# A graph attention layer on one core: 58 tiles of raw node rows are gathered while the node table is built

## The chip, the core and the metric

One core of a Trainium2 chip. The metric is device microseconds of one execution. The kernel before takes 4131.94 us, the median of three runs (4130.94 to 4132.53). Five engines work side by side, each through its own list of instructions in order: PE (TensorE, matrix products), DVE (VectorE), ACT (ScalarE), POOL (GpSimd) and SP (SyncE, which only issues transfers here). They wait for one another by semaphores.

## The reference

There are 12,500 nodes with 128 features and 412,500 edges, sorted by their target, with 64 features each; 4 heads of 32.

```python
h = relu(layernorm(x))                       # 12500 x 128
h = h @ W_node.T;  e = edge_attr @ W_edge.T  # per head: 32 columns
att = sum(concat(h[src], h[dst], e) * a)     # one logit per edge and head
att = where(att > 0, att, 0.2 * att)
m = maximum(segment_max(att, dst), 0)
ex = exp(att - m[dst])
denom = segment_sum(ex, dst) + (num_edges - deg) * exp(-m)
out = x + segment_sum(ex / denom[dst] * h[src], dst)
```

## The kernel before, in words

**The table.** The kernel first builds, in device memory, a `table` with one row of 144 numbers per node: for each head the 32 projected features, two columns of ones and the node's own logits towards source and target. Then it walks over the edges in 66 batches (`NBT`) of 7 chunks of 896 edges (49 tiles of 128 edges each; less in the last batch), gathers the table row of each edge's source node, works out the weights, and sums the weighted rows per target on PE.

**The lead-in** (`lead_in`, L432) builds the table from 98 tiles of 128 nodes (`NB`), loaded and written in 14 groups (`sizes`, L305), mostly of 9 tiles; a unit is 3 tiles of a group. A group's x rows are loaded by SP (`load_rows`, L307). DVE takes the statistics of each tile (`measure`, L329), combines them per group (`combine`, L334, four instructions), ACT takes the root (`root`, L344), and DVE makes the scale and the shift (`deviate`, L349, two instructions). A unit is then normalized (`normalize`, L355: its first tile on ACT, the other two on POOL), turned on PE (`turn`, L368), taken through ReLU on the way out of PSUM (`keep_turned`, L373: the first tile on ACT, the other two on DVE), multiplied with the weights on PE (`project`, L382), copied out by ACT (`keep_rows`, L387), and POOL sets its columns of ones (`set_ones`, L394). A group's rows are written to the table by an ACT transfer (`write`, L398), and POOL copies its target logits (`keep_logits`, L402).

The order of these steps on each engine comes from a list scheduler at the end of `lead_in`: a `Step` has an engine, a duration and a lag in ns, the steps it stands behind, and a rank; the step that can start first by these numbers is emitted next, the rank deciding between equals. The numbers only set the order; the engines wait by semaphores.

Behind the lead-in stand `keep_near` (L406: the target logits are turned and written to device memory) and `chunk_ranges` (L513), in which DVE works out, for all chunks at once, where each begins.

**The batches** (L1089 on). `gather` (L660) issues one indirect transfer on POOL per tile of 128 edges: 128 rows of the table, found through a column of the batch's index tile `ends` (`index`, L232). The gathered rows lie in `hs`, one of four buffers (`RING`); the first two, `opening` and `second`, are set apart before the lead-in, the other two come after it. Batches 0 and 1 are gathered without any wait but that for the table and the indices; from batch 4 on a small memset (`gate`, L663) in front of a batch's gathers waits until PE has done the sums of the batch four before it. DVE waits for a batch's rows in `weigh` (L738; a wait on a counting semaphore), makes the logits and weights, marks targets (`mark`, L719), and multiplies the rows by the weights in `scatter` (L846), whose matrix products sum them. `choose` (L628) picks each edge's target logits, and `begin` (L706) makes the edge features' part of the logits on PE.

Ahead of the lead-in POOL sets constants (L186 to L215: `logits`, `pen_sb`, `marks`, `carry`).

Of the kernel before, what the change touches and what calls it, by code (L numbers as in the profile page):

```python
# [49 lines left out]
ACTS = 1  # L50
# [76 lines left out]
def kernel(  # L127
# [58 lines left out]
    nc.gpsimd.memset(logits, 0.0)  # L186
    pen_sb = const.tile([R, 2, CE + 1], F32, name="pen_sb")
    nc.gpsimd.memset(pen_sb, 0.0)
# [4 lines left out]
    nc.gpsimd.memset(lowest, 0.0)  # L193
    nc.gpsimd.memset(highest, float(NQ))
    for b0, n, b in parts():
        c = chunk_of(b + 1)
        if c < NCH:
            nc.gpsimd.memset(lowest[:, c:c + 1], float((b0 + n) * (P // W)))
    for b in range(NBT):
        if b == NBT - 1 or base_of(b + 1) > base_of(b):  # L200
            c = chunk_of(b + 1) - 1
            nc.gpsimd.memset(highest[:, c:c + 1], float(base_of(b) + WQ - 2))
    for at in sorted({base_of(b) for b in range(NBT)}):
        of = [b for b in range(NBT) if base_of(b) == at]
        nc.gpsimd.memset(bases[:, chunk_of(of[0]):chunk_of(of[-1] + 1)], float(at))

# [6 lines left out]
    nc.gpsimd.memset(carry_m, 0.0)  # L213
    carry = const.tile([P, AW - 1], F32, name="carry")
    nc.gpsimd.memset(carry, 0.0)  # L215
# [22 lines left out]
    with (  # L238
# [6 lines left out]
    ):  # L245
        wn = p1.tile([P, D], F32, name="wn")
# [60 lines left out]
        def load_rows(b0, n):  # L307

            s = Rows()
            s.b0, s.n = b0, n  # L310
# [4 lines left out]
            if full < n:  # L315
                nc.vector.memset(s.x[:, full, :], 0.0)
                rest = N - (b0 + full) * P
                nc.sync.dma_start(s.x[:rest, full, :], x[(b0 + full) * P:N, :])
            s.stats = p2.tile([P, XB, 2, 3], F32, name="stats", bufs=5)
# [34 lines left out]

        def normalize(u, own):  # L355
# [3 lines left out]
            for i in own:  # L359
                k = slice(u.i0 + i, u.i0 + i + 1)  # L360
                if i < ACTS:
                    nc.scalar.activation(u.hn[:, i, :], s.x[:, k, :].rearrange("p b d -> p (b d)"), AF.Identity,
                                         scale=s.rstd[:, k], bias=s.shift[:, k])
                else:
                    nc.gpsimd.tensor_scalar(u.hn[:, i, :], s.x[:, k, :].rearrange("p b d -> p (b d)"),
# [7 lines left out]
        def keep_turned(u, own):  # L373
            if u.hT is None:
                u.hT = p2.tile([P, XS, P], F32, name="hT", bufs=5)
            if own[0] < relu_acts(u):
                for i in own:
                    nc.scalar.activation(u.hT[:, i, :], u.pt[:, i, :], AF.Relu)
                return
            nc.vector.tensor_scalar(u.hT[:, own[0]:u.m, :], u.pt[:, own[0]:u.m, :], 0.0, None, op0=OP.max)  # L380
# [6 lines left out]
        def keep_rows(u):  # L387
            s = u.s
            if u is s.units[0]:
                s.rows = p3.tile([P, XB, ROW], F32, name="rows", bufs=4)  # L390
# [1071 lines left out]
```

## Time and profile before

| what | value |
|---|---|
| median of 3 runs | 4131.94 us |
| the profiled execution | 4131.72 us |
| its span, first to last instruction | 4129.9 us |
| mean granted TensorE clock | 0.658 |
| busy: DVE, POOL, PE, ACT | 58%, 75%, 33%, 11% |
| indirect gathers on POOL | 3223, mean 947 ns, from 63.3 us on |
| moved by the DMA engines | 457.10 MB, mean 111 GB/s |

The rows of the profile are read so: a group's row has its line, engine, operation, what it writes and reads, its count, then the busy time and the mean ns of one, then the idle time of the engine just before these instructions and what ended it. A timeline's row begins with the start and the duration in us. Engines with a small q (SPq, ACTq) are the issuing of transfers. "issue" is time in which an engine waited for nothing that the profile shows.

### The profile page before, as it was taken

Reading aid. Unit: us, or ns where it says so; the run is one execution under the profiler, and the core shown is the slowest. Engines: PE = TensorE matmul, PEld = TensorE weight load, DVE = VectorE, ACT = ScalarE, POOL = GpSimd, SP = SyncE. Lnnn points to the kernel's source line nnn. Section 1 sums busy time; section 2 is a strip of 40 time slices with the busy share of each in tenths; the row PEclk is TensorE's granted clock in tenths of the full one; section 3 lists DMA queues with packets and bytes.
Section 4 is the critical chain, followed back from the end, with each engine's and each line's share of the span. In section 5 each row is a group of like instructions: output and inputs, shape, how many; then the busy total and the mean of one; then the engine's idle time right before and its main releaser. Section 6 shows DMA issues by size and latency. Waiting matters only on the chain. (4 is left out here: it accounts for less than half of the span.)

```text
span 4129.9 us, 18410 instructions
## 1 busy us (share of the span) xinstructions
PE 1360.4 (33%) x3375; PEld 538.8 (13%) x3375; DVE 2390.1 (58%) x3503; ACT 461.0 (11%) x669; POOL 3100.1 (75%) x3457
## 2 busy tenths in 40 slices
PE   5333133233233323323323313323323332332332
PEld 4111011011011111101101101101111110110111
DVE  7446556556556556745655754654665654665576
ACT  4001101101101101101110110110110110110011
POOL 6777777777777777777777777777777777777775
PEclk8666666566566666666666666656666666666665
DMA  7433343343344344333434333434434434434432
GB/s 205 124 114 101 108 116 106 106 113 112 99 114 117 96 113 119 102 107 114 102 107 119 106 108 110 108 106 113 115 99 115 117 92 112 119 99 114 119 102 61
DMA packets 417255, 457.10 MB, mean 111 GB/s; under 512 B 240614, under 2 KB 324794, under 8 KB 417132
## 3 DMA queue, kind: packets, MB, share of 16 engines
q0 software_dynamic: 103136, 237.83, 21.8%
q1 hardware_dynamic: 200288, 165.86, 14.0%
q10 hardware_dynamic: 113708, 52.17, 4.6%
q14 instruction: 95, 0.78, 0.1%
q8 instruction: 28, 0.46, 0.0%
HBM read 406.51 MB, written 49.05 MB: 110 GB/s over the span
## 5 line engine op out<-in xcount | busy, mean ns | idle before, releaser
L667 POOL DMA_INDIRECT hs<-table,ends x3223 | 3053.1, 947 | 978.1 <-issue 974.7
L857 PE MATMUL pa<-hs,hot 128*128 128x504 f32 x1820 | 929.5, 676 | 2665.9 <-DVE hs L852 2665.9
L765 DVE TENSOR_TENSOR logits<-hs,pick 128x196 f32<-128x196 f32 x65 | 32.4, 499 | 1495.0 <-DVEq L684 1495.0
L857 PEld LDWEIGHTS pa<-hs,hot 128*128 128x128 f32 x1820 | 397.7, 223 | 3189.9 <-issue 3158.9
L852 DVE TENSOR_TENSOR hs<-hs,exr 128x1848 f32<-128x1848 f32 (+1 forms) x130 | 451.6, 3516 | 0.0
L780 ACT ACTIVATE both<-a 32x224 f32<-32x224 f32 (+2 forms) x268 | 103.2, 385 | 2591.6 <-DVE a L778 2589.3
L715 PE MATMUL z<-eft,wa 128*32 128x512 f32 (+1 forms) x792 | 320.0, 547 | 6.5 <-DMA eft<-in_ef 6.5
L642 DVE COPY_PREDICATED pick<-more,pick 128x1568 f32<-128x1568 int32 (+3 forms) x260 | 253.6, 975 | 8.9
L642 DVE COPY_PREDICATED pick<-more,lw 128x3136 f32<-128x3136 int32 x65 | 241.0, 3707 | 9.6 <-ACT pick L626 3.9
L626 ACT COPY pick<-lw 128x3136 f32<-128x3136 f32 x65 | 182.4, 2806 | 11.5 <-ACTq L684 10.0
L964 DVE TENSOR_TENSOR acc<-acc,up 128x70 f32 x461 | 105.2, 228 | 66.0 <-issue 51.1
L775 DVE TENSOR_TENSOR_SCAN up<-pen_sb,z 32x896 f32<-32x896 f32 (+1 forms) x67 | 133.6, 1994 | 2.3
L777 DVE TENSOR_TENSOR_SCAN m<-pen_sb,up 32x896 f32<-32x896 f32 (+1 forms) x67 | 132.6, 1979 | 2.3
L735 DVE TENSOR_TENSOR hot<-exr,key 128x1568 f32<-128x1568 f32 x65 | 116.4, 1791 | 2.3
L770 DVE TENSOR_TENSOR up<-z,zst 32x224 f32<-32x224 f32 (+2 forms) x268 | 104.3, 389 | 13.8
L715 PEld LDWEIGHTS z<-eft,wa 128*32 128x32 f32 x792 | 79.7, 110 | 242.1 <-issue 234.9
L782 DVE SCALAR_TENSOR_TENSOR both<-pen_sb,up 32x224 f32<-32x224 f32 (+2 forms) x268 | 100.1, 374 | 4.3
L894 ACT COPY r<-turned 128x245 f32<-128x245 f32 x65 | 41.4, 638 | 337.5 <-ACTq L684 294.4
L774 DVE TENSOR_TENSOR z<-up,a 32x896 f32<-32x896 f32 (+1 forms) x67 | 72.3, 1079 | 2.3
L778 DVE TENSOR_TENSOR a<-z,m 32x896 f32<-32x896 f32 (+1 forms) x67 | 71.7, 1070 | 2.3
L773 DVE TENSOR_SCALAR a<-up 32x896 f32<-32x896 f32 (+1 forms) x67 | 71.3, 1064 | 2.3
L712 PE MATMUL z<-eft,wa 128*64 128x512 f32 (+1 forms) x132 | 64.6, 572 | 21.6 <-DMA eft<-in_ef 21.6
(182 smaller groups left out, 901.5 us busy)
## 6 DMA issues: line engine op xcount, KB each, us to landing
eft<-in_ef SPq DMA_DIRECT2D x33, 1792.0 KB
hs<-table,ends POOLq DMA_INDIRECT x3223, 2.5
eft<-in_ef SPq DMA_DIRECT2D x33, 1344.0 KB
wide<-stage ACTq DMA_DIRECT2D x65, 504.0 KB, 2.9
lw<-near SPq DMA_DIRECT2D x461, 64.0 KB
pen_sb<-pens SPq DMA_DIRECT2D x66, 98.1 KB
xg<-in_x SPq DMA_DIRECT2D x52, 112.0 KB
table<-rows ACTq DMA_DIRECT2D x8, 648.0 KB
```

The lines of the kernel that those rows point to most:

```text
L626: nc.scalar.copy(s.pick[:, :, :s.chunks, :], lw[:, None, :s.chunks, :n].to_broadcast([P, T, s.chunks, n]))
L642: nc.vector.copy_predicated(s.pick[:, :, :s.chunks, :n], bit[:, :, :, None].to_broadcast([P, T, s.chunks, n]), more)
L667: load = nc.gpsimd.indirect_dma_start(out=s.hs[:, t * CB + q, :], out_offset=None, in_=table[:, :], in_offset=bass.IndirectOffsetOnAxis(ap ...
L715: s.made = own_half(s, nc.tensor.matmul(s.z[:, part], wa3[:, j + s.b % 2 * (SB + 1), :], s.eft[:, j, part], start=False, stop=(j == NEXT - ...
L735: nc.vector.tensor_tensor(s.hot.rearrange("p t q r -> p (t q) r"), rows_ps[:, None, :].to_broadcast([P, T * CB, W]), key[:, :, None].to_br ...
L770: on_half(s, nc.vector.tensor_tensor(grouped(up, g), grouped(s.z, g), zst[g * R:(g + 1) * R, t0:t1, :], op=OP.add))
L775: on_half(s, nc.vector.tensor_tensor_scan(up[:, e0:e1], s.pen[:, e0:e1], z, 0.0, op0=OP.add, op1=OP.max))
L777: nc.vector.tensor_tensor_scan(mp[:, ::-1], s.pen[:, e1:e0:-1], up[:, e0:e1][:, ::-1], 0.0, op0=OP.add, op1=OP.max)
L780: nc.scalar.activation(both[g * R:(g + 1) * R, 0, t0:t1, :], grouped(att, g), AF.Exp)
L852: nc.vector.tensor_tensor(rows, rows, ex_ps[:, t0:t1, :CB * H, None].to_broadcast([P, t1 - t0, CB * H, HB]), op=OP.mult)
L857: scattered[s.b] = nc.tensor.matmul(wide_ps[:, g, :], s.hot[:, t, g * NEXT:g * NEXT + SB, :].rearrange("p q r -> p (q r)"), flat[:, at:at ...
L964: nc.vector.tensor_tensor(sums, sums, put[:, i0 + i, :, :], op=OP.add)
```

## The change

The rows of the whole first batch (49 tiles) and of the first 9 tiles of the second (`RAW = (49, 9)`) are no longer gathered from the table. POOL gathers the edges' raw x rows (512 bytes of x in place of 576 bytes of the table) straight into the two `hs` buffers as soon as the first index tile is there, while the table is being built. These 58 tiles then go through the lead-in in place, as 7 further groups behind the table's 14: they are normalized, turned, projected, and `keep_rows` writes the 144 columns over the raw rows. They are not written to the table, and they have no target logits to keep.

POOL has no other share in the lead-in any more: the normalization of its two tiles goes to ACT, but for the first tile of each third unit, which DVE takes; ReLU is all on DVE, three tiles in one instruction; the ones and the logits' copies go to DVE. POOL's constants move behind its raw gathers. The first use of the weights moves into a step of its own, `prepare`. `gather` skips the tiles that are there already, and `weigh` of batch 0 has no wait on a counting semaphore.

```diff
-ACTS = 1
+RAW = (T * CB, XB)
...
+    def set_constants():
+        nc.gpsimd.memset(carry, 0.0)
...
+        early = [index(0)]
+        raw = [pool.tile([P, T * CB, ROW], F32, name="hs") for pool in (opening, second)]
+
+        def gather_raw(k):
+            for i in range(RAW[k]):
+                nc.gpsimd.indirect_dma_start(
+                    out=raw[k][:, i, :D], out_offset=None, in_=x[:, :],
+                    in_offset=bass.IndirectOffsetOnAxis(ap=early[k][:, i % CB, 0, i // CB:i // CB + 1], axis=0))
+
+        gather_raw(0)
...
+            at = b0 - NB
+            if at >= 0:
+                s.rows = raw[0][:, at:at + n, :] if at < RAW[0] else raw[1][:, at - RAW[0]:at - RAW[0] + n, :]
+                s.x = s.rows[:, :, :D]
+                return parted(s)
...
+        def of_vector(u):
+            return (u.s.b0 + u.i0) // XS % 3 == 0 and u.m == XS
...
-                if i < ACTS:
+                if i or not of_vector(u):
                     nc.scalar.activation(u.hn[:, i, :], s.x[:, k, :].rearrange("p b d -> p (b d)"), AF.Identity,
                                          scale=s.rstd[:, k], bias=s.shift[:, k])
                 else:
-                    nc.gpsimd.tensor_scalar(u.hn[:, i, :], s.x[:, k, :].rearrange("p b d -> p (b d)"),
+                    nc.vector.tensor_scalar(u.hn[:, i, :], s.x[:, k, :].rearrange("p b d -> p (b d)"),
                                             s.rstd[:, k], s.shift[:, k], op0=OP.mult, op1=OP.add)
...
+        def keep_turned(u):
+            u.hT = p2.tile([P, XS, P], F32, name="hT", bufs=5)
+            nc.vector.tensor_scalar(u.hT[:, :u.m, :], u.pt[:, :u.m, :], 0.0, None, op0=OP.max)
...
-            nc.gpsimd.memset(rows.rearrange("p b (h k) -> p b h k", h=H)[:, :, :, HD:HD + 2], 1.0)
+            nc.vector.memset(rows.rearrange("p b (h k) -> p b h k", h=H)[:, :, :, HD:HD + 2], 1.0)
...
-            nc.gpsimd.tensor_copy(tn[:, s.b0:s.b0 + s.n, :],
+            nc.vector.tensor_copy(tn[:, s.b0:s.b0 + s.n, :],
...
+        tables = len(sizes)
+        sizes += [min(XB, n - i) for n in RAW for i in range(0, n, XB)]
...
-            if len(groups) == len(sizes):
+            if len(groups) == 3:
+                early.append(index(1))
+                gather_raw(1)
+                set_constants()
+            if len(groups) == tables:
                 early.extend(index(b) for b in range(2, AHEAD))
...
+                if g >= tables:
+                    steps["landed", g] = Step("gathered", 1250 * n, 5000, [], g, lambda: None)
+                    steps["load", g] = Step("none", 0, 0, behind + [("landed", g), ("load", g - 1)], g, load_next)
...
-        s.hs = rings[s.b % RING].tile([P, T * CB, ROW], F32, name="hs")
+        s.hs = raw[s.b] if s.b < 2 else rings[s.b % RING].tile([P, T * CB, ROW], F32, name="hs")
...
-                if t < tiles_of(s.c0 + q):
+                if t < tiles_of(s.c0 + q) and t * CB + q >= (RAW[s.b] if s.b < 2 else 0):
                     s.tiles.append((t, q))
```

How the order on the engines moves, at three places. First POOL at the end of the lead-in, before (`tn` holds the target logits, `rows` a group's table rows, `hs` a batch's gathered rows):

```order
L403 COPY tn<-rows 128x24
L396 MEMSET rows 128x12x2
L403 COPY tn<-rows 128x12
L396 MEMSET rows 128x8x2
L403 COPY tn<-rows 128x8
L667 DMA hs<-table,ends 128x144 x196
L663 MEMSET gate 128x1
L667 DMA hs<-table,ends 128x144 x49
```

And POOL with the change, from its second iota on:

```order
L164 IOTA pid_c 128x1
L253 DMA hs<-in_x,ends 128x128 x58
L201 MEMSET carry 128x34
L202 MEMSET carry_m 128x1
L203 MEMSET pen_sb 32x1794
L204 MEMSET logits 128x224
```

```order
L217 MEMSET marks 1x21
L217 MEMSET marks 1x6
L699 DMA hs<-table,ends 128x144 x138
L695 MEMSET gate 128x1
L699 DMA hs<-table,ends 128x144 x49
```

The normalizations, ones and copies are gone from POOL; 58 gathers of x and then the constants stand in their place, and of the 196 gathers in front of the first gate 138 are left. The raw gathers also carry waits, here with the semaphores' names (`DMAHW` counts plain transfers, `DMASW` POOL's; eight of each are used in turn):

```order
L253 DMA hs_131<-in_x,ends_129 128x128 [waits DMAHW1_49]
L253 DMA hs_131<-in_x,ends_129 128x128 x7
L253 DMA hs_131<-in_x,ends_129 128x128 [waits DMASW0_49]
L253 DMA hs_131<-in_x,ends_129 128x128 [waits DMASW1_49]
L253 DMA hs_131<-in_x,ends_129 128x128 [waits DMASW2_49]
```

From the ninth on each waits for the transfer that used its semaphore last, the one eight before. Next DVE in the middle of the table, for about one group of nine, before (`stats`, `tot`, `dif`: statistics; `shift`, `rstd`: scale and shift; `pt`, `hT`: a turned unit before and after ReLU):

```order
L351 RECIPROCAL rstd_475<-rstd_475 128x9
L353 SCALAR_TENSOR_TENSOR shift_495<-tot_424,rstd_475 128x9
L337 TENSOR_TENSOR tot_497<-stats_272 128x18
L339 TENSOR_TENSOR dif_499<-stats_272 128x9
L340 SCALAR_TENSOR_TENSOR dif_499<-dif_499 128x9
L341 TENSOR_TENSOR dif_499<-dif_499,tot_497 128x9
L332 BN_STATS stats_315<-xg_313 128x6 x6
L380 TENSOR_SCALAR hT_529<-pt_518 128x256
L332 BN_STATS stats_315<-xg_313 128x6 x3
L380 TENSOR_SCALAR hT_551<-pt_535 128x256
```

And with the change (`hn`: a normalized unit):

```order
L374 RECIPROCAL rstd_532<-rstd_532 128x9
L376 SCALAR_TENSOR_TENSOR shift_547<-tot_488,rstd_532 128x9
L360 TENSOR_TENSOR tot_553<-stats_327 128x18
L362 TENSOR_TENSOR dif_555<-stats_327 128x9
L363 SCALAR_TENSOR_TENSOR dif_555<-dif_555 128x9
L364 TENSOR_TENSOR dif_555<-dif_555,tot_553 128x9
L391 TENSOR_SCALAR hn_559<-xg_302,rstd_532,shift_547 128x128
L355 BN_STATS stats_384<-xg_382 128x6 x3
L417 MEMSET rows_526 128x12x2
L355 BN_STATS stats_384<-xg_382 128x6 x3
L417 MEMSET rows_526 128x12x2
L401 TENSOR_SCALAR hT_582<-pt_569 128x384
```

A normalization of one tile and the ones have come in between, and each ReLU is on 384 elements in place of 256. Last, DVE towards the table's end, with the change, where the first raw groups (`hs_131` is batch 0's buffer) come in:

```order
L355 BN_STATS stats_997<-hs_131 128x6 x3
L417 MEMSET rows_1085 128x12x2
L360 TENSOR_TENSOR tot_1093<-stats_997 128x18
L362 TENSOR_TENSOR dif_1095<-stats_997 128x9
L363 SCALAR_TENSOR_TENSOR dif_1095<-dif_1095 128x9
L364 TENSOR_TENSOR dif_1095<-dif_1095,tot_1093 128x9
L417 MEMSET rows_1085 128x12x2
L401 TENSOR_SCALAR hT_1102<-pt_1087 128x384
L424 COPY tn_205<-rows_1085 128x24
```

The statistics of raw tiles stand between the table's last units: 21 raw statistics and 11 small operations of raw groups come ahead of the last table unit's ones; all the rest of the raw tiles' work on DVE comes behind it.

116 lines of the change are left out of this document (57 added, 59 removed).

## The prediction

> **What bounds the kernel now.** I read the profile's busy table and its costliest groups first, to see which engine is full; then the one line in which POOL is busy, with its waits; then the timeline of POOL at its start and its end. First the busy shares, the gathers' group and DVE's wait for the gathers:
>
> ```profile
> PE 1360.4 (33%) x3375; PEld 538.8 (13%) x3375; DVE 2390.1 (58%) x3503; ACT 461.0 (11%) x669; POOL 3100.1 (75%) x3457
> L667 POOL DMA_INDIRECT hs<-table,ends x3223 | 3053.1, 947 | 978.1 <-issue 974.7
> L765 DVE TENSOR_TENSOR logits<-hs,pick 128x196 f32<-128x196 f32 x65 | 32.4, 499 | 1495.0 <-DVEq L684 1495.0
> ```
>
> POOL's 75% is deceptive: between two gathers there are 0.30 us of issue that count as idle. DVE, the only other candidate, stands 1495 us waiting for gathered rows, 23 us in each of 65 batches. The gathers' own waits with the starts of the first and the last, then two neighbours in POOL's timeline (first number: start, second: duration, us):
>
> ```profile
> L667 POOL DMA_INDIRECT hs<-table,ends x3223: 940/944/1867, 63.3 to 4097.5; - x190
>   issue: 974.7, 3221
>   DMA table<-rows: 3.1, 1
>   DVEq L909: 0.3, 1
> DMA to landing us min/median/max: 2.4/2.5/5.9
> 4085.01 0.94 POOL L667 DMA_INDIRECT hs<-table,ends  x1 [0.30 <-issue]
> 4086.26 0.94 POOL L667 DMA_INDIRECT hs<-table,ends  x1 [0.30 <-issue]
> ```
>
> One gather each 1.25 us, 3223 of them without a pause from 63.3 to 4097.5, and 32.4 us of tail to the end of the span at 4129.9. So the span is: start of the first table gather, plus the number of gathers behind it times 1.25, plus the tail. Everything else matters only through these. The start is where POOL's two lead-in jobs end and the table has landed:
>
> ```profile
> 1.39 0.12 POOL L164 IOTA pid_c<- 128x1 int32 x1
> 1.47 0.27 POOL L186 MEMSET logits<- 128x224 f32 x1
> 6.01 0.12 POOL L215 MEMSET carry<- 128x34 f32 x1
> 59.94 0.19 POOL L403 COPY tn<-rows 128x8 f32<-128x8 f32 x1
> 63.26 1.16 POOL L667 DMA_INDIRECT hs<-table,ends  x1 [3.13 <-DMA table<-rows]
> ```
>
> **What goes: 58 gathers.** Behind the table only 3165 gathers are left. 58 x 1.2495 (800 gathers take 1000 us in the middle, below) = **72.5 us less**. They are the same instruction on 128 rows, of 512 instead of 576 bytes; I take the same price, since the 0.94 did not move with what the memory did.
>
> **What comes: a later first table gather.** Call its start S, 63.3 before. Two chains race for it.
>
> *POOL's chain.* It begins when the first index tile lands. No row shows that landing. Issues and a consumer of a load that was issued at the same moment:
>
> ```profile
> 0.74 0.41 ACTq L247 DMA_DIRECT2D wn<-in_w_node  x1
> 0.75 0.88 SPq L234 DMA_DIRECT2D ends<-in_ends  x2
> 2.17 0.49 ACTq L252 DMA_DIRECT2D ac<-in_a_col  x1
> 3.18 0.45 PE L491 MATMUL pw<-ident,wn 128*128 128x128 f32 x1 [3.18 <-DMA wn<-in_w_node]
> 6.14 0.17 DVE L488 TENSOR_TENSOR a_diag<-ac,tsel 128x12 f32<-128x12 f32 x1 [1.91 <-DMA ac<-in_a_col]
> ```
>
> The weights needed 2.44 us, the slow little load 3.97; so the index is there between 3.2 and 4.7, and I take 3.3, by the weights, which are nearer in size and moment. Then 58 gathers: 72.5, to 75.8. Then the constants, which were done by 6.13 and now stand behind: 6.13 - 1.47 = 4.7, to 80.5. Added is what DVE takes from POOL while both run. The worst such stage of before is the one in which DVE works out the chunk ranges; windows of the gathers alone, there and in the middle, then one collision of it:
>
> ```profile
> 63.00:125.00 62.00, 48.03 (x46) 0.56 0.57 174
> 1000.00:2000.00 1000.00, 756.10 (x800) 0.66 0.40 109
> 71.34 1.85 POOL L667 DMA_INDIRECT hs<-table,ends  x1 [0.30 <-issue]
> 71.29 1.08 DVE L295 TENSOR_TENSOR xg<-xg 128x895 int32<-128x895 int32 x1
> 72.41 0.63 DVE L296 TENSOR_SCALAR rows<-xg 128x895 f32<-128x895 int32 x1
> ```
>
> A gather took 1.044 there and 0.945 in the middle, where DVE's operations between SBUF tiles are few and small: 0.1 more per gather. The gather at 71.34 ends at 73.19, just behind the two DVE operations on 895 elements. In the lead-in DVE's operations of that sort are on 9 to 128 elements, far nearer to the middle's. Bounds: 0, and 58 x 0.1 = 5.8 us at the worst stage's mean. I take 2. With 0.2 for the last wait, POOL's chain gives **S = 82.7**, between 80.6 and 88.
>
> The Trainium skill, "SBUF — State Buffer", "Who interferes with whom", states that VectorE in a two-port mode, or with two SBUF inputs against a reader, and GpSimd exclude one another for a whole instruction. The pair at 71.34 agrees. The rule speaks against the change, which puts 58 gathers and some 95 such DVE operations (14 groups x 5 for the statistics, 11 normalizations, 14 copies) into one stage; at full price, about 0.19 us each, it would make 18 us instead of 2.
>
> *The table's chain.* POOL's share of the lead-in goes to DVE and ACT. Busy time of the engines by stretch (PE, PEld, DVE, ACT, POOL), and the groups of DVE and POOL in the lead-in:
>
> ```profile
> 6.00:18.00 12.00, 7.44 (x34) 6.04 (x34) 10.47 (x58) 5.63 (x15) 4.88 (x17) 1.00 0.94 249
> 18.00:48.00 30.00, 28.51 (x190) 23.54 (x190) 27.54 (x134) 24.19 (x72) 21.43 (x72) 1.00 0.87 246
> 48.00:58.00 10.00, 8.54 (x63) 7.73 (x64) 6.86 (x30) 8.11 (x24) 6.55 (x24) 1.00 0.55 166
> L332 DVE BATCH_NORM_STATS2 stats<-xg 128x6 f32<-128x128 f32 x98 | 21.2, 278 | 0.0
> L380 DVE TENSOR_SCALAR hT<-pt 128x256 f32<-128x256 f32 x33 | 13.3, 417 | 4.6 <-ACT hT L378 2.9 <-PE pt L371 1.3
> L362 ACT ACTIVATE hn<-xg,shift,rstd 128x128 f32<-128x128 f32 x33 | 15.6, 492 | 2.0 <-DVE shift L353 1.1 <-POOL hn L365 0.8
> L378 ACT ACTIVATE hT<-pt 128x128 f32<-128x128 f32 x32 | 8.7, 276 | 3.2 <-DVE hT L380 2.0 <-PE pt L371 1.0
> ```
>
> DVE is the fullest: 10.5 + 27.5 + 6.9 = 44.9 us of 52. For what it takes over the nearest DVE rows are these (a small memset, small and large SBUF sources, a large PSUM source):
>
> ```profile
> 3.72 0.07 DVE L270 MEMSET ext<- 128x12 f32 x1
> 349.51 0.19 DVE L952 COPY carry<-up 128x34 f32<-128x34 f32 x1
> 91.35 0.38 DVE L541 TENSOR_SCALAR xg<-xg 128x468 int32<-128x468 int32 x1
> 86.46 0.65 DVE L526 COPY xg<-pn 128x468 f32<-128x468 f32 x1
> ```
>
> The third tile of each ReLU: (0.65 - 0.42)/212 x 128 = 0.14, x 32 = 4.5. Ones: 33 x 0.1 = 3.3. Logits: 14 x 0.19 = 2.7. Normalizations: 11 between 0.19 and 0.38, nearer the first, 2.2. Raw work that the order puts ahead of the last table unit: 21 statistics x 0.216 = 4.5 and 11 small operations x 0.19 = 2.1. Sum 19.3, so 64.2 us of DVE work. At the old filling of 86% that is 74.4 us, at the 92% of the middle stretch 69.9; from 6.0 the last table unit is ready at 76 to 80.5. From there to the gather it was 63.26 - 59.94 = 3.3. So **S = 79 to 84** by the table. ACT (37.9 us in the same stretches) loses 8.7 and gains 54 normalizations at 0.49, 26.5, at most since pairs overlap: 55.7, below DVE.
>
> POOL's 82.7 lies in the upper half of the table's span. The later of the two sets S; I take **S = 83.0, +19.7 us**.
>
> **What lies beside.** DVE and ACT still have 37 raw tiles to finish then, and everything behind the lead-in on DVE moves back. DVE's rest: 37 x 0.216 + 38 x 0.19 + 20 x 0.56 + 20 x 0.1 = 28.4, by 0.86: 33, so until about 112. The first batch's chain of before, from the turned logits to the end of its sums on PE:
>
> ```profile
> 60.91 1.05 ACT L412 COPY turned<-pn 98x512 f32<-98x512 f32 x1 [1.12 <-PE pn L410]
> 114.72 2.12 PE L715 MATMUL z<-eft,wa 128*32 128x384 f32 x6
> 130.80 0.50 DVE L765 TENSOR_TENSOR logits<-hs,pick 128x196 f32<-128x196 f32 x1 [20.32 <-DVEq L684]
> 148.06 15.14 PE L857 MATMUL pa<-hs,hot 128*128 128x504 f32 x28 [18.27 <-DVE hs L852]
> ```
>
> Without the wait for rows (batch 0's are in place) it is 55.9 + 32.4 = 88 us, so PE ends at about 200. POOL asks for that buffer after 138 gathers, at 83 + 172.5 = 255: 55 us of slack, and DVE, with 23 us spare per batch, is back in step by batch 3. So POOL should not stop. Nothing changes in the tail. I add 1 us for collisions of the raw work with the first table gathers.
>
> **Sum**: 4129.9 - 72.5 + 19.7 + 1.0 = 4078.1 of span; the profiled execution took 4131.7, 1.8 more than its span, and the median of the runs is 4131.9. **4080 us**, 1.3% faster.
>
> **Rivals.** (1) *The table is late*: DVE and ACT, now both nearly full and in a fixed order, fill worse than before, say 80%: 80 + 6 + 3.3 = 89.5, 4086.5. For it speaks that 86% was reached with POOL's help; against it, that the middle stretch had 92%. 20%. (2) *Collisions* at the worst stage's price or more: S from 86 to 92, 4083 to 4089; against it speak the 800 gathers at 0.945. At the full price named above the Trainium skill's page "SBUF — State Buffer" would have S = 98.7 and 4096. 12%. (3) *Less is lost*: no collisions and the table not waited for, S = 80.6, 4076.5. 6%. (4) *Lanes*, the other side: in the built order each raw gather from the ninth on waits for the landing of the one eight before. At 5.9 us, the longest landing seen, this costs nothing, as eight take 10 us. It decides from 10 us on; at landings of 20 us a gather would take 2.5, the 58 145 us, S = 155, 4152. Even needs S = 135.8, landings of 17.6 us. For it: the DMA engines are 0.87 to 0.94 busy in the lead-in; against it: three times the longest landing is needed. 3%. (5) *DVE does not come back in time* and POOL stops at batch 4: needs 55 us more than worked out; or the raw groups get ahead of the table in the schedule, which the order denies but for 6.6 us. 2%, about even.
>
> **How the numbers follow.** Forecast (S 81.5 to 84.5, 4078 to 4082) 57%. The range, 4076 to 4091, takes in (1), most of (2) and (3). What a measurement can tell from no change is 0.2%, 8 us: faster 0.95, same 0.02, slower 0.03.
>
> **What would show it.** In the changed profile: the first raw gather at about 3.3, 58 of them at 1.25 to 1.3 us, the first table gather at 83 with its releaser (POOL itself: forecast; a table DMA: rival 1), raw gathers of 1.1 and more (2), waits for gather landings between them (4), POOL idle at a gate (5). A first table gather beyond 92, or gaps behind it, would make the prediction wrong.

## The result, and the profile after

The changed kernel takes **4073.43 us** (median of 4 runs, 4072.53 to 4074.66) against 4131.44 for the kernel before: a ratio of 0.9862 (95% interval 0.985 to 0.9874), 1.4% faster. The forecast was 4080, with a range of 4076 to 4091. The direction and the mechanism came as foretold; the time lies 2.6 us below the range. The profiled execution took 4074.66 us, 1.9 more than its span of 4072.8.

In five of the six later groups of runs, each group on one chip, the kernel before itself took 4742 to 4787 us (one of these chips gave 4135 to 4137 seven minutes later), so each run below is compared with the kernel before in its own group. The two conditions are called *free* (before: 4131 to 4137; the measurement above is one) and *held* (before: about 4755); the expectations below take them for two kinds of chips.

The page of the changed kernel, busy shares and the two groups to be set against those of before:

```profile
PE 1394.6 (34%) x3549; PEld 563.4 (14%) x3549; DVE 2426.0 (60%) x3707; ACT 503.8 (12%) x770; POOL 3066.5 (75%) x3345
...
L699 POOL DMA_INDIRECT hs<-table,ends x3165 | 2997.6, 947 | 957.5 <-issue 957.3
...
L798 DVE TENSOR_TENSOR logits<-hs,pick 128x196 f32<-128x196 f32 x65 | 32.4, 498 | 1383.3 <-DVEq L716 1383.1
```

POOL is as busy as before and DVE still waits for gathered rows, 1383 us where it was 1495: the same engine bounds the kernel. The two kinds of gathers by their lines (duration min/median/max in ns, first and last start), the table's first, then the raw ones with what POOL waited for ahead of them:

```profile
L699 POOL DMA_INDIRECT hs<-table,ends x3165: 940/944/1859, 80.6 to 4041.4; - x198
...
  issue: 957.3, 3164
  DVE key L765: 0.2, 1
```

```profile
L253 POOL DMA_INDIRECT hs<-in_x,ends x58: 940/944/1107, 3.1 to 74.6; - x58
...
  issue: 17.4, 57
  DMA ends<-in_ends: 1.6, 1
...
DMA to landing us min/median/max: 3.0/4.0/6.6
```

No gather waited for a landing or a gate, and one for DVE, 0.2 us. POOL from the last raw gather to the first table gather:

```profile
74.61 0.94 POOL L253 DMA_INDIRECT hs<-in_x,ends  x1 [0.30 <-issue]
75.56 0.14 POOL L201 MEMSET carry<- 128x34 f32 x1
...
75.66 1.60 POOL L203 MEMSET pen_sb<- 32x1794 f32 x1
...
79.31 0.92 POOL L217 MEMSET marks<- 1x42 f32 x15
80.57 0.95 POOL L699 DMA_INDIRECT hs<-table,ends  x1 [0.35 <-issue]
```

The first table gather stands right behind POOL's own constants: its releaser is "issue", not a transfer of the table. The last of those was issued earlier, here on ACT's queue:

```profile
71.77 0.37 ACTq L420 DMA_DIRECT2D table<-rows  x1
```

Busy time by stretch, in the order PE, PEld, DVE, ACT, POOL:

```profile
6.00:18.00 12.00, 8.05 (x28) 6.16 (x29) 9.74 (x54) 6.24 (x17) 9.20 (x10) 1.00 1.06 268
18.00:48.00 30.00, 23.03 (x144) 19.12 (x142) 25.88 (x137) 24.98 (x67) 22.74 (x24) 1.00 0.93 246
48.00:72.00 24.00, 19.84 (x131) 16.02 (x131) 21.67 (x117) 22.03 (x59) 18.00 (x20) 1.00 0.85 231
```

DVE did 57.3 us of work in the 66 us of the table, 87%. Where the 57.1 us between the two spans came from: the first table gather starts 17.3 later (63.26 to 80.57); from the first to the last table gather it took 4034.2 before (63.26 to 4097.50) and 3960.9 now (80.57 to 4041.43), 73.4 less; from the last gather's start to the end of the span it took 32.4 before and 31.4 now, 1.0 less. 17.3 - 73.4 - 1.0 = -57.1.

### The profile page after: what moved, and what is told of

Its sections match the earlier page's. It is cut to its first block, busy times and chain, and to the rows that moved or that the text cites. A ratio compares the mean times of both kernels' runs of the same rounds, so it can differ in the third digit from the quotient of the medians.

```text
span 4072.8 us, 19016 instructions
## 1 busy us (share of the span) xinstructions
PE 1394.6 (34%) x3549; PEld 563.4 (14%) x3549; DVE 2426.0 (60%) x3707; ACT 503.8 (12%) x770; POOL 3066.5 (75%) x3345
## 5 line engine op out<-in xcount | busy, mean ns | idle before, releaser
L699 POOL DMA_INDIRECT hs<-table,ends x3165 | 2997.6, 947 | 957.5 <-issue 957.3
L798 DVE TENSOR_TENSOR logits<-hs,pick 128x196 f32<-128x196 f32 x65 | 32.4, 498 | 1383.3 <-DVEq L716 1383.1
L811 DVE TENSOR_TENSOR a<-z,m 32x896 f32<-32x896 f32 (+1 forms) x67 | 71.7, 1070 | 2.3
```

The lines of the kernel that those rows point to most:

```text
L699: load = nc.gpsimd.indirect_dma_start(out=s.hs[:, t * CB + q, :], out_offset=None, in_=table[:, :], in_offset=bass.IndirectOffsetOnAxis(ap ...
```

## The experiments

The theory: POOL's own chain (first index, raw gathers at 1.25 us, constants) sets the start S of the table gathers, the table is ready some us ahead of it, and a raw gather costs POOL just what a table gather does. The rival: the table's chain on DVE and ACT sets S, or the gathers collide with DVE's work.

### Four variants, and a condition that had not been foreseen

`consts_first` calls `set_constants()` ahead of `gather_raw(0)` instead of behind the raw gathers. `consts_dve` gives all the constants to DVE, behind the lead-in; `consts_dve_raw67` has more raw tiles besides, and `raw52`, `raw67` and `raw91` change nothing but their number:

```diff
+        set_constants()
         gather_raw(0)
...
                 gather_raw(1)
-                set_constants()
```

```diff
-        nc.gpsimd.memset(carry, 0.0)
+        nc.vector.memset(carry, 0.0)
...
         lead_in()
+        set_constants()
```

```diff
-RAW = (T * CB, XB)
+RAW = (T * CB, 2 * XB)    # raw67; raw52: (T * CB, 3); raw91: (T * CB, 42)
```

Expected of `consts_first`:

> POOL's constants (4.7 us) stand ahead of the raw gathers again, as they did before the change, where 1.6 us of POOL's wait for the first index hide them. If POOL's own chain sets the first table gather, the first raw gather moves from 3.10 to about 6.2, the 58th ends at 78.7, and the first table gather starts at 79.0 in place of 80.57: 1.6 us less, about 4071.8. If the table's last rows set it (rival: the chain on DVE and ACT is ready at about 80.5), it stays at 80.5 with a table transfer as releaser, 4073.4.

Of `consts_dve`:

> POOL's constants go to DVE, behind the lead-in. If POOL's chain sets the start, the first table gather comes right behind the last raw one, at 3.1 + 72.5 + 0.3 = 75.9, 4.7 us less, about 4068.7, as long as the table has landed: its last transfer was issued at 71.77, and 3.3 us later is 75.1. DVE's 4 to 6 us more behind the lead-in cost nothing, since POOL asked for batch 0's buffer 64 us after PE was done with it. Rival, the table at 79 to 84 as the prediction had it: a start of 79 or more with a table transfer as releaser, 1.6 us less at the most, 4071.8 or above.

Of `consts_dve_raw67`:

> The same, with 18 tiles of the second batch gathered raw in place of 9. If each raw tile only trades a raw gather for a table gather on POOL, the start is 75.9 + 11.25 = 87.1, with 9 gathers less behind it, and the time is that of the kernel with 9 tiles, 4068.7; it is a little better than that one if there the table was still late. Rival, every raw tile costs something elsewhere (DVE's raw work behind the table, collisions): 1 us and more above the kernel with 9 tiles.

Of `raw52`:

> 3 tiles of the second batch raw in place of 9: POOL's chain ends at 80.6 - 7.5 = 73.1, and what is seen is when the table itself is ready. By its last transfer's issue at 71.77 and 3.3 us behind it: a start of about 75.1 with a table transfer as releaser, 6 gathers more behind it (7.5 us): 2 us more than the changed kernel, about 4075.4. Rival, the table's chain at 79 to 84 as predicted, so that both chains were late together: start 80.6, 7.5 us more, 4081. Without any wait for the table it would be 73.1 and the same time.

Of `raw67`:

> 18 tiles of the second batch raw in place of 9, constants as in the change. POOL's chain alone: start at 80.6 + 11.25 = 91.8, 9 gathers less behind it, no difference (4073.4, within 0.5 us). Rival, the raw tiles' work on DVE and ACT or collisions cost something per tile: at the 0.1 us per gather of the chunk ranges' stage 1 us more, and a start later than 91.8.

Of `raw91`:

> 42 tiles of the second batch raw, 91 in all. POOL's chain: start at 80.6 + 41.25 = 121.8, 33 gathers less behind it, no difference (4073.4, within 1 us). DVE has 33 x 0.77 = 25 us more raw work, 30 us by its filling, so PE ends batch 0 at about 223 in place of 193.7, still 30 us ahead of POOL's first gate at 253. So the raw gathers only fill the time until the table is there; more of them earn nothing. Rival, each tile costs or earns: 0.1 us per gather for collisions is 3 us more; a stop at the first gate would show as a wait of POOL for PE.

All six met the held condition, so none tells anything on its expectation's times. One part of them can be read: in `consts_first` POOL's raw gathers run from 6.3 to 77.8, as expected. Next, the changed kernel itself beside the kernel before:

> The changed kernel itself once more, beside the kernel before. Eight variants of it ran on two chips on which the kernel before took 4744 to 4783 us in place of 4131, and all but two of them were 2% slower than it there. On a chip of the first kind: 4073 against 4131, first table gather at 80.6, tail 31.4 to 32.4. On a chip of the second kind, if the variants' stalls belong to the raw gathers and not to their edits: about 4840 against 4750, with the first table gather at 130 to 140 and waits of 10 to 25 us on PE, ACT and DVE in the lead-in while raw gathers run.

The measured times and starts (us; the ratio is to the kernel before in the same group of runs; the gap is from the last raw gather's start to the first table gather's):

| kernel | last raw gather | first table gather | gap | time | ratio and interval |
|---|---|---|---|---|---|
| raw52 | 67.1 | 130.1 | 63.0 | 4843.2 | 1.0164 (1.0119 to 1.0208) |
| after_again | 74.4 | 137.0 | 62.6 | 4840.7 | 1.0158 (1.0122 to 1.0193) |
| consts_dve | 74.6 | 136.8 | 62.2 | 4856.8 | 1.0187 (1.0131 to 1.0243) |
| consts_first | 77.8 | 138.5 | 60.7 | 4853.1 | 1.0181 (1.0131 to 1.0230) |
| consts_dve_raw67 | 85.8 | 147.4 | 61.6 | 4860.0 | 1.0211 (1.0153 to 1.0269) |
| raw67 | 85.9 | 149.1 | 63.2 | 4838.2 | 1.0199 (1.0142 to 1.0256) |
| raw91 | 115.7 | 179.6 | 63.9 | 4861.0 | 1.0220 (1.0175 to 1.0265) |

So in the held condition the change makes the kernel **1.6% slower**. What the column of gaps says is plain: however many raw gathers there are, the table is ready 61 to 64 us behind the last of them, nearly the whole time it takes to build. While POOL gathers raw rows, the lead-in all but stands still. Busy time by stretch in `after_again`, in the order of above, then the granted clock:

```profile
18.00:48.00 30.00, 2.85 (x11) 2.10 (x10) 2.19 (x10) 4.23 (x10) 22.64 (x24) 1.00 0.28 74
```

DVE did 2.2 us of work where it did 25.9 in the free condition, at the same granted clock of 1.00. Where the lead-in stands, in `after_again` (PE, ACT and DVE in the lead-in; line 406 is the projection, 397 the turning, 413 ACT's copy of the projected rows, 401 the ReLU):

```profile
19.38 1.81 PE L406 MATMUL ph<-wall,hT 128*128 128x144 f32 x6 [0.97 <-DVE hn L391]
...
20.98 0.85 PE L397 MATMUL pt<-ident,hn 128*128 128x128 f32 x3
...
43.86 0.52 ACT L413 COPY rows<-ph 128x432 f32<-128x432 f32 x1 [15.12 <-remote]
...
52.26 0.56 DVE L401 TENSOR_SCALAR hT<-pt 128x384 f32<-128x384 f32 x1 [24.53 <-remote]
...
52.96 1.78 PE L406 MATMUL ph<-wall,hT 128*128 128x144 f32 x6 [31.14 <-issue]
...
54.53 1.49 PE L397 MATMUL pt<-ident,hn 128*128 128x128 f32 x6
...
69.06 0.52 ACT L413 COPY rows<-ph 128x432 f32<-128x432 f32 x1 [23.52 <-remote]
...
76.76 0.56 DVE L401 TENSOR_SCALAR hT<-pt 128x384 f32<-128x384 f32 x1 [22.68 <-issue]
```

PE had projected by 21.2 and turned by 21.8; ACT copied at 43.9 and DVE took the ReLU at 52.3, 23 and 30 us behind what they waited for. (The trace shows the end of PE's work and the start of the waiting instruction; that it is the signal between them that is late is the reading of this text.) In the other direction nothing is late: DVE ends at 52.82, PE starts at 52.96. The next pair: PE done at 54.7 and 56.0, ACT at 69.1, DVE at 76.8. In the free condition these are waits of about 1 us (11.2 us in 10 for ACT's copies). The same shows in the batches, where PE's sums go to ACT (line 899) and POOL's gate (line 695) waits for PE. Waits of `after_again` (us, times, longest):

```profile
ACT stage L899 <- remote: 1113.6, 38, 49.9
...
POOL gate L695 <- remote: 448.5, 37, 21.9
...
POOL gate L695 <- PE pa L890: 120.1, 1, 120.1
```

POOL stops at 38 of 62 gates, for 569 us in all, the first time, at 429, for 120; in the free condition it stopped at none. A gather's own time is unchanged (944 ns at the median). Of the 760 us between the two spans (4833.3 against 4072.8) the gates make 569, the later start 56, and a longer tail 119 (150 from the last gather on, in place of 31). In this condition POOL is not the bound, and the gathers taken from it earned nothing.

### The offload alone, and the ones back on POOL

`no_raw`: nothing is gathered raw, and batch 0 waits for its rows as before.

```diff
-RAW = (T * CB, XB)
+RAW = (0, 0)
...
-               *([s.ends[:, :, :, :]] if s.b < NBT - 1 else [])) if s.b else None
+               *([s.ends[:, :, :, :]] if s.b < NBT - 1 else []))
```

> POOL's share of the lead-in is on DVE and ACT as in the change, but nothing is gathered raw: all 3223 gathers come behind the table. The last table transfer came at 71.77 with 6.6 us of raw work ahead of it on DVE; without that, at 87% filling, at about 64.2, and landed at 67.5. So the first table gather starts at about 67.5 against 63.3 before: 4 us slower than before, about 4135.7. Then moving POOL's share costs 4 us by itself and the raw gathers earn the other 62. Rival, the table's chain as the prediction worked it out (64.2 us of DVE work less 6.6, at 86 to 92%): 68.6 to 73 and landed at 72 to 76, 9 to 13 us slower, 4140 to 4144.

4761.3 us, ratio 1.0012 (0.9988 to 1.0036): no difference to be measured. Its lead-in has no gathers beside it and runs undisturbed (ACT's copies wait 6.0 us for PE in 6 waits), so its start may be read: 72.5, against 63.3 with POOL's help. The releaser in the trace is the transfer of the target logits (`near<-turned`); the table's last transfer was issued at 68.9, so with the 2.8 us that `raw_plain` (below) shows from issue to start the table itself was ready at about 71.7. My 67.5 was wrong and the rival's 72 to 76 right: the offload by itself moves the start by 8 to 9 us.

`ones_pool`: the ones by POOL again.

```diff
-            nc.vector.memset(rows.rearrange("p b (h k) -> p b h k", h=H)[:, :, :, HD:HD + 2], 1.0)
+            nc.gpsimd.memset(rows.rearrange("p b (h k) -> p b h k", h=H)[:, :, :, HD:HD + 2], 1.0)
```

> One line of the change undone: the columns of ones are set by POOL again, in the place that the order of the program gives them. They stand behind the 58 raw gathers and the constants in POOL's list, so no group's rows can be written before 80.6. With four buffers of rows the lead-in stands still after four groups (27 tiles) from about 25 us on, and does the other 71 tiles from 80.6 on, at the 0.58 us per tile of before: first table gather at 120 to 127, about 40 to 47 us slower than the changed kernel, 4113 to 4120. Rival, only POOL's time counts: 54 memsets of 0.1 us, 5 us slower, 4079.

The first table gather starts at 143.5, later than expected, and the lead-in stands still until 80 as it should: a normalization on ACT waits 71.7 us for POOL's ones. So an instruction's place in the list counts, not its 0.1 us. But the time is 4759.5, ratio 1.0012 (0.9984 to 1.0040), against 1.0158 for `after_again`: some 70 us less in place of 40 more. So in the held condition an early start of the table gathers is not what decides, as the next three show too.

### What holds PE's results back

Three ways to keep the raw tiles' place and change what POOL does in it. `pool_busy` leaves the fetching of the raw rows out, `raw_plain` their choice by index:

```diff
-                nc.gpsimd.indirect_dma_start(...)
+                nc.gpsimd.memset(raw[k][:, i // 7 * 7:i // 7 * 7 + 7, :], 0.5)      # pool_busy
+                nc.sync.dma_start(raw[k][:, i, :D], x[i * P:(i + 1) * P, :])        # raw_plain
...
                 nc.gpsimd.indirect_dma_start(...)
+                nc.gpsimd.memset(spare, 0.0)                                       # raw_spaced, 1330 elements
```

> Each of the 58 raw gathers is replaced by a memset of 1008 elements on POOL (about 1 us, so POOL is busy just as long); what is left out is the fetching of these rows, which hold a constant. On the chips where the kernel before takes 4750, PE's results reached ACT and DVE 6 to 30 us late in the lead-in while raw gathers ran. If the gathers cause that, it is gone: the ReLU and the copy of the rows wait under 1 us each for PE, the table's last transfer is issued at 72 to 76 and the first table gather starts at 65 to 80, by POOL's chain or the table. If POOL's being busy is enough to cause it, the start stays at 130 to 140.

> The raw rows come by plain transfers of SP, five tiles behind each group's load, from the first 7424 rows of x in place of the edges' sources (so the fetching by index is left out); POOL has nothing to do but its constants. The bytes moved in the lead-in are the same. If the instructions of POOL's gathers hold PE's results back, the lead-in runs undisturbed and the first table gather shows when the table itself is ready: 73 to 77 with a table transfer as releaser (its last transfer was issued at 71.8 and took about 3.3), far from the 79 to 84 of the prediction's second chain. If the traffic of the raw rows holds them back, 130 to 140 as with gathers.

> Behind each raw gather POOL sets 1330 elements (1.2 us), so that gathers are issued at half the rate and the 58 take 142 us, until about 146. If a pause of 1.2 us lets PE's results through, the lead-in runs nearly undisturbed beside it: rows and ReLU wait 1 to 3 us for PE at most, the table is done by 90 to 100, and the first table gather comes from POOL's chain at about 150. If the pauses are too short, the waits of 6 to 30 us last as long as raw gathers do, the table is built mostly behind them, and the start is at 190 to 210.

All three in one group, held. In `pool_busy` 58 memsets of 0.94 us kept POOL busy without a pause until 58.3, and nothing was held: the table gathers start at 76.0. In `raw_plain` the same bytes came by plain transfers, and nothing was held: POOL's first table gather waits for the table's last transfer, issued at 70.10, and shows when the table is ready:

```profile
72.91 1.11 POOL L699 DMA_INDIRECT hs<-table,ends  x1 [66.79 <-DMA table<-rows]
```

In `raw_spaced` the gathers are there, 2.34 us apart in place of 1.25, and nothing is held: the rows' last copy is at 76.1, the start at 142.4 by POOL's chain, the time 4749.4, ratio 0.9992 (0.9965 to 1.0020). So neither POOL's being busy nor the traffic is enough; it takes **gathers issued back to back**. `pool_busy` and `raw_plain` still take 4781.4 and 4798.7, ratios 1.0056 (1.0024 to 1.0088) and 1.0084 (1.0051 to 1.0118): their table gathers start early and run back to back beside the raw tiles' remaining work, the chunk ranges and the first batches, which fits, and the first gate stops POOL for 116 us at 364 and 362. In `no_raw`, `raw_spaced` and `ones_pool` the first gate stands at 323, 332 and 342, with 0, 11 and 9 us of waiting; in `after_again` at 429. From there on all these kernels take 4410 to 4440 us (median less first gate): what sets them apart in the held condition lies ahead of the first gate.

The record shows one thing more, a pace. From the first gate to the last gather are 3027 gathers; the held kernels take 1.404 to 1.413 us for each, with or without raw gathers, where the changed kernel in the free condition takes 1.250. The raw gathers of `after_again` end at 75.36, but POOL's next small memsets come up to 1.4 us apart until 84.45 (in the free condition they follow on each other), and just there ACT is let go, and DVE with it (at 84.46, after 6.5 us):

```profile
84.45 0.48 POOL L214 MEMSET marks<- 1x1 f32 x13 [0.61 <-issue]
84.55 0.52 ACT L413 COPY rows<-ph 128x432 f32<-128x432 f32 x1 [14.78 <-remote]
```

From the first raw gather (3.10) to 84.45 it is 58 times 1.403 us; by the same memsets the effect of 52 raw gathers ends at 76.26, of 67 at 97.05 and of 91 at 130.69, again 1.402 to 1.403 for each gather. So in the held condition something takes 1.40 to 1.41 us per gather; POOL issues one each 1.25, and what it is ahead must be worked off before signals come on time again. `raw_spaced`, at 2.34, never gets ahead. This reading fits every held run; what takes the time is not shown.

### Short pauses behind every gather

A memset of 1, 128 or 256 elements on POOL behind each gather, raw or from the table:

```diff
+    pause = const.tile([P, 128], F32, name="pause")
...
                     in_offset=bass.IndirectOffsetOnAxis(ap=early[k][:, i % CB, 0, i // CB:i // CB + 1], axis=0))
+                nc.gpsimd.memset(pause, 0.0)
...
                 by_itself(load, f"rows{s.b}", row_sems, row_done, s.b % ROWSEMS)
+            nc.gpsimd.memset(pause, 0.0)
```

> The changed kernel with a memset of one element (0.1 us) on POOL behind every gather, raw or from the table. It may vanish in the 0.30 us of issue between two gathers, as the gate's memset did. If any other instruction between two gathers lets PE's results through, the waits of 6 to 30 us are gone, the first table gather comes at 80 to 88 and the time is 4073 plus 3165 times 0 to 0.05: 4073 to 4230. If POOL has to pause for longer, about 4840, and 130 to 140 for the start.

> The same with 128 elements (0.2 us). The pitch grows by 0.10 to 0.15: if that lets PE's results through, the first table gather starts at 86 to 92 and the time is 4073 + 3223 x 0.10 to 0.15, 4400 to 4560. If not, 4840 or above.

> The same with 256 elements (0.3 us). The pitch grows by 0.20 to 0.25: if that lets PE's results through, the first table gather starts at 92 to 98 and the time is 4073 + 3223 x 0.20 to 0.25, 4720 to 4880, set by POOL alone with no stop at the gates. If not, the gates still stop POOL and the start is beyond 130.

These runs were in the free condition (before: 4136.5), so what they test is the sum of the prediction. Measured: 4080.8, ratio 0.9866 (0.9837 to 0.9895); 4362.9, ratio 1.0548 (1.0517 to 1.0579); 4702.4, ratio 1.1369 (1.1336 to 1.1402). The pitch (first to last start by the lines below, over 3164 steps; 1.2519 in the changed kernel) grew by 0.002, 0.089 and 0.195, less than the memsets last (0.12, 0.22 and 0.33), since part of each lies in the 0.30 of issue; so the last two times are below what I had given. The 0.002 is no more than the gathers' own time, 946 ns at the median in place of 944, and the kernel before was 5 us slower in this group as well: a memset of one element costs nothing that these runs can tell. The start tells more. Table gathers by line, of 1, 128 and 256 elements:

```profile
L701 POOL DMA_INDIRECT hs<-table,ends x3165: 940/946/1854, 80.6 to 4048.1; - x198
```

```profile
L701 POOL DMA_INDIRECT hs<-table,ends x3165: 950/953/1653, 85.7 to 4329.5; - x198
```

```profile
L701 POOL DMA_INDIRECT hs<-table,ends x3165: 950/953/1713, 92.0 to 4669.7; - x198
```

The start moves by 58 times the pitch's growth: 80.6 + 58 x 0.089 = 85.8 and 80.6 + 58 x 0.195 = 91.9, measured 85.7 and 92.0. If the table set it, the first of these steps would have vanished in the wait. **POOL's own chain sets S**, shown in the condition of the measurement. And time put on POOL alone comes out at the end: the start and the train together grow by 3222 times 0.0894 and 0.1950 us, 288 and 628, and the spans grew by 287.1 and 627.3, with tails 1.0 shorter.

### The last three

Pauses of one element behind the raw gathers alone (`consts_dve_pause`, `raw91_pause`), or behind all gathers with nothing raw (`no_raw_gap1`); the edits are those above, combined.

> POOL's constants on DVE behind the lead-in, and a memset of one element behind each raw gather, which was free where it was measured. Where the kernel before takes 4131 to 4136: if POOL's chain sets the start, the first table gather comes at 3.1 + 72.5 + 0.3 = 75.9, 4.7 us earlier than in the changed kernel and just behind the table (ready at 73 to 76): 4068.7 to 4069, against 4073.4. If the table's chain were at 79 to 84 as in the prediction, 4072 or above with a table transfer as releaser. Where the kernel before takes 4750: a start at 76 to 80 if a pause of 0.1 us lets PE's results through, 137 as without it if not.

> 91 tiles raw in place of 58, with the same pause, constants as in the change. Where the kernel before takes 4131 to 4136: first table gather at 80.6 + 41.25 = 121.8, 33 gathers less behind it, no difference to the changed kernel: 4073.4 within 1 us, if a raw tile only trades one gather for another and DVE's 30 us more raw work stay inside its slack of 64 us at the first gate. If raw tiles cost something each (0.1 us by the chunk ranges' stage), 3 us more. Where it takes 4750: a start at 122 if the pause is enough, 180 as without it if not.

> The offload alone, nothing gathered raw, with a memset of one element behind every gather (in the changed kernel that made 7.4 us, 4080.8). Where the kernel before takes 4131 to 4136: with the table ready at about 73 less the raw work of 6.6 us on DVE at 87%, the first table gather starts at 66 to 70 against 80.6, with 58 gathers more behind it: 4080.8 - 10.6 to 14.6 + 72.5 = 4139 to 4143, so that the offload by itself costs 3 to 7 us against 63.3. By the prediction's table chain, 71 to 76, 4144 to 4149. Where it takes 4750: below 4400 if the pause of 0.1 us lets PE's results through in the batches, 4750 to 4760 if not.

Held again (before: 4755.9). 4840.1, ratio 1.0178 (1.0144 to 1.0212), with the start at 133.4; 4865.4, ratio 1.0216 (1.0177 to 1.0256), start 173.4: one element behind the raw gathers is not enough. It helps a little: the pitch of the raw gathers becomes 1.38, and the table gathers start 52 and 45 us behind the last of them, in place of 62 and 64. `no_raw_gap1` took 4663.3, ratio 0.9804 (0.9769 to 0.9839), more than the 4400 that I had set as the mark for free signals, but 2.0% below the kernel before in this condition, where `no_raw` was even. Its pauses are not as short as they look. POOL's timeline in it:

```profile
2003.64 0.94 POOL L701 DMA_INDIRECT hs<-table,ends  x1
2005.47 0.10 POOL L708 MEMSET pause<- 128x1 f32 x1 [0.90 <-remote]
2005.72 0.94 POOL L701 DMA_INDIRECT hs<-table,ends  x1
2006.87 0.10 POOL L708 MEMSET pause<- 128x1 f32 x1 [0.21 <-POOL pause L708]
```

The memset writes the tile that the one before it wrote, and waits for that one's signal; here this signal, from POOL to POOL, is late too, by 0.2 us in 435 waits and by up to 2.3 in 370 more that are put down as "remote" (343.6 us; `after_gap1` in the free condition had neither). POOL never stops at a gate, the pitch is 1.41 in place of 1.25, the pace found above, and DVE waits for gathers again. So it is not PE's signals alone that come late while gathers are issued.

What makes the condition stays open. One chip showed both, so it is not the chip alone; nor is it the granted clock: 0.629 to 0.643 as the mean of the profiled held runs against 0.644 in `after_gap256`, which was free, and 1.00 in both conditions from 18 to 48 us, where the lead-in stands still. And of the versions without constants on POOL, none met the free condition: that `consts_dve` would reach 4068.7 there, and that more raw tiles are neutral there, was not measured.

## Why the prediction was right in kind and wrong in size

1. **POOL bounds the kernel; the span is S + gathers behind it + tail.** Right for the measurement, and shown by the pauses: time added to POOL alone comes out in the span to within 1 us. Wrong for the held condition, which nothing in the profile of before announced; there the same edit costs 1.6%.
2. **58 gathers less: 72.5.** The train of gathers became 73.4 shorter. The 1.0 that I added for collisions of the raw work with the first table gathers did not come, and 0.9 more came off: together 1.9 of the miss.
3. **POOL's chain, 82.7.** Measured 80.57. The first raw gather started at 3.10 (I had 3.3 for its index), and 3.10 + 58 x 1.2495 = 75.57 is where the constants began (75.56). That sum has an issue of 0.30 behind the last gather, which was not paid, so of the **2 us for collisions 0.3 came**: the first gather took 1.11 us and one other 1.07. The constants and the last wait took 5.0 (I had 4.9). With the 0.3 that I rounded up to S = 83.0, this makes 2.4 of the miss.
4. **The rule against the change.** By the Trainium skill, "SBUF — State Buffer", section "Who interferes with whom", of a DVE operation and a GpSimd instruction that need the ports the two share, the one issued first shuts the other out for its whole length. In my sum DVE was the first every time, for 18 us. The trace does not show that for these gathers: median 944 ns, two of 58 over 0.97, 0.3 us in all beside the normalizations and the statistics' combinations.
5. **The table's chain, 79 to 84.** Too late by 4 to 9 us. Its last transfer was issued at 71.77, and by the 2.8 us from issue to start in `raw_plain` it had landed near 74.6: POOL's chain had 6 us in hand, where I thought both arrived together. To 44.9 us of busy time I had added 19.3 by full durations, 64.2; DVE was busy 57.3, at the 87% that I had assumed. By groups its work did grow by 17.5 (51.6 from 6 to 58 us before, 69.1 from 6 to 72 now), but the engine's busy time by 12.4: neighbours overlap at their ends, as a memset of the ones of 0.08 us does with the ReLU ahead of it. The raw work ahead of the last table unit, 6.6 in my sum, moved the table's last transfer by 1.2 (70.1 in `raw_plain`, 68.9 in `no_raw`).
6. **The first batch.** PE ended it at 193.7 (about 200 foretold) and POOL asked for its buffer at 257.8 (255): 64 us of slack, no stop, in the free condition. In the held one this very slack was gone, and POOL stood 120 us there.
7. **The tail, "nothing changes".** 1.0 less. In the tail DVE waits for ACT's copy of the turned sums, here before and after:

```profile
4095.56 0.38 DVE L928 TENSOR_SCALAR mc<-r 128x7 f32<-128x7 f32 x1 [1.51 <-ACT r L894]
```

```profile
4038.56 0.17 DVE L962 TENSOR_SCALAR mc<-r 128x7 f32<-128x7 f32 x1 [0.49 <-ACT r L928]
```

The copy waits for small transfers that read the sums back, and the copy came 1.9 us behind their last issue in place of 2.9. The tails of the three kernels with pauses are 31.2, 30.4 and 30.4: a term that moves by up to 2 us over these profiles, and I had treated it as fixed.

The **step that failed** is the price of collisions, "I take 2" on POOL's chain and "I add 1 us" behind it: the runs showed 0.3 and none, which is 2.7 of the miss of 6.6. With it went "the later of the two sets S; I take S = 83.0": the table was not near. The start came where rival (3), "less is lost", had put it, 80.6, with a chance of 6%; the worst-stage price was given too much weight against rows (the 800 gathers at 0.945) that said zero.

That alone would have stayed inside the range. Its lower end, 4076, was rival (3)'s 4076.5, a sum in which the train and the tail were exact; the train came out 0.9 shorter, the tail 1.0, and the median lies 1.2 below the profiled execution. These 3.1 us, for which the range had nothing, put the time below it. In all, S makes 2.4, the train 1.9, the tail 1.0 and the median 1.2: 6.5 of the 6.6.

## What to carry to other kernels

Work that an engine can do without waiting (here gathers of raw rows) fills the time in which it would wait for a result; the gain is what it saves behind (here 73.4 us) less what it delays ahead (here 17.3, by the work handed to DVE and ACT and by POOL's own chain), not the number of instructions moved. Price a collision by the rows that are most like the new pair, and give the case "it costs nothing" its full share when those rows say so. A range needs room for the terms that are held fixed in every rival. A kernel whose engines hand results to one another beside an engine that issues transfers back to back can depend on how fast those signals get through: look at the waits behind finished work before trusting that the fullest engine is the bound.

## What the runs showed of the hardware

- In the held condition ACT and DVE started 6 to 30 us behind the end of PE's work while indirect gathers were issued each 1.25 us, and on time when they were 2.34 us apart, when POOL ran memsets of 0.94 us in their place, and when plain transfers moved the same rows. From DVE to PE it took 0.14 us all the same. The held kernels make one gather each 1.40 to 1.41 us.
- In the free condition a memset of one element between two gathers costs no pitch that can be told (0.002 us at most): it lies in the 0.30 of issue. 128 elements cost 0.089, 256 cost 0.195.
- Where POOL and DVE ran side by side, either could be the one to lose. Beside DVE's operations on 895 elements single gathers took 1.75 to 1.86 us (113 to 128 us in the changed kernel). A normalization of 128 elements on DVE, 0.34 us at the median of the table's tiles, took 2.49 beside POOL's memset of 1.60 us at 75.66 (one case, not tried apart):

```profile
75.49 2.49 DVE L391 TENSOR_SCALAR hn<-hs,rstd,shift 128x128 f32<-128x128 f32 x1
```

- A raw gather of 512-byte rows landed in 4.0 us at the median beside the table's traffic, a table gather in 2.6; both take POOL 944 ns.
